# Two kinds of loads, of the mask and of the first part's maxima, moved from SyncE's queue to GpSimd's, in a two-layer transformer kernel

## The chip, the cores and the metric

The kernel runs on one core of a Trainium2 chip. The metric is the device time of one execution in microseconds (us). Three runs of the kernel before gave 3211.42, 3217.47 and 3217.95 us; the median is 3217.47.

The engines go by the names of the profile: PE is TensorE (matmuls), DVE is VectorE, ACT is ScalarE, POOL is GpSimd, SP is SyncE (no arithmetic, it begins transfers). Each runs its own list of instructions strictly in order and waits for the others by semaphores. L1034 is line 1034 of the kernel.

## The reference

The inputs are x (2048 rows of 256), a context of 1601 rows of 256, an integer mask of 2048 x 2048, and weights. Two layers follow each other, both with 16 heads of width 16:

```python
# layer 0 (x0, x1: the two halves of the rows; c: the context, whose first two rows give shifts, scales, gates)
x0 = x0 + gate * mha(mod(ln(x0)))          # self attention inside each half
x1 = x1 + gate * mha(mod(ln(x1)))
ox = attend(q of x0, k, v of x1);  oy = attend(q of x1, k, v of x0)
x  = x + gate * (proj(ox), proj(oy))       # cross attention between the halves
x  = x + gate * mlp(mod(ln(x)))            # gelu, width 1024
# layer 1
scores = where(mask == 0, -1e9, q @ k.T / 4)
x = layernorm(x + softmax(scores) @ v @ ow + ob)        # masked self attention over all 2048 rows
x = layernorm(x + mha(x, context, context))             # attention to the 1601 context rows
x = layernorm(x + relu(x @ w1 + b1) @ w2 + b2)
```

So there are four attentions, which the kernel calls stages 0 to 3: self, cross, masked, context. Only stage 2 has a mask.

## The kernel before

**Units and steps.** The rows of x make four blocks of 512 queries. Each stage runs through the blocks in the order of `ORDER` (stage 0: 0, 1, 2, 3; the others: 2, 3, 0, 1), and each block through four groups of four heads. One stage, block and group is a *unit*. Keys lie in two slots of 1024 (`slot`). The keys of a unit are walked in tiles of 128, two head pairs each; each such pair is a *step* of the main loop in `stream` (L1356 on). A step with one slot of the masked stage takes some 2 us, so a unit with 16 steps takes 32 us or more and one with 32 steps about 62.

Stage 2 begins when the cross stage has made only half of the keys. Its first block, block 2 (`SPLIT`), is therefore done in two *parts*: part 0 with the first slot of keys for groups 0 to 3, then part 1 with the second slot for groups 0 to 3. That makes eight units of 16 steps, and the results of the two parts are put together by `compare`, `invert_both`, `fetch_first` and `divide` (L1285 to L1324). These eight units run at about 1217 to 1575 us in the profiled execution; the last block of the cross stage, with its MLP, is finished beside them, and so are the four chunks of context (`chain_context`, L784), whose keys and values stage 3 needs.

**What a unit does.** Ahead of its turn, `maxima` (L1065) makes the scores once with queries on the partitions (PE, L1094 and L1099) and takes their maxima over the keys (DVE, L1109; in stage 2 L1102, which adds a row of the mask's bias first). `negated` and `as_rows` (L1116, L1129) turn the negative maxima into rows: PE L1133, then ACT L1138 writes `nm`. In its turn, `weights_of` (L1158) makes the scores with keys on the partitions: in stage 2 the bias, transposed, by L1173, the products by L1180, minus the maxima by L1187, then the exponential on ACT (L1194). `values_of` (L1198) multiplies by the values (L1211), `copy_sums` takes the sums out (L1243) and SP brings them to their places (L1249, L1258). Some steps later the reciprocal of the sums goes through memory (L1280, L1282) and `divide` multiplies on POOL (L1289, and L1292, L1293 where there are two parts).

**The order.** All five engines keep the order in which the code emits instructions (`manual_schedule`, L88); nothing is reordered. Work that lies beside the units is put in by hand: `later` is a list of functions with the number of steps until they are due, `background` a list of generators (the chains of normalization, projections, MLP) that are advanced one piece a step, `transfers` a list of loads of keys and values of which each step issues one (`load_ready`, L980).

**The two kinds of loads that the change touches.**

- `mask_rows` (L1016) loads 128 rows by 512 integers of the mask (256 KB) into `raw`, a tile with two buffers, and POOL turns it into a bias in bf16 (L1035). The load is L1034. There are 64 such pairs: eight for block 2 and slot 0, begun by `mask_part(0)` near the end of the cross stage; eight for block 2 and slot 1, begun by `mask_part(1)` during the down projection of the last cross MLP; and 16 for each of the blocks 3, 0 and 1, emitted between the maxima of the fourth group of the block before (L1082 to L1086), two by two or one by one.
- `as_rows` (L1129): for the eight units of block 2 alone, right after `nm` has been written, eight small loads (2 KB each, from two rows of `nm` per head to 32 partitions, L1145) bring the maxima into `mh`, and four steps later DVE adds the two halves (`add`, L1149 to L1151; the result serves `compare`).

**What else lies on POOL.** Sums with the gates and residuals of the layer (L586, L588; L599 later), the power of -1/2 in the normalizations (L400), the second part of the norms (L610), copies of weights (L230), a memset of a column of ones in each tile of values `v` (L506), the products of `divide` (L1289 to L1293). **What else lies on SP:** nearly all other transfers; for the steps of the prediction, the stores of keys and queries that have been split into two floats, `hi` and `lo` (L495), the stores of values (L542 to L550, each of which needs the memset and the sums of DVE, L523), the loads of keys (L933) and values (L949, L956), of queries (L1001) and of the context chunk (L793).

The tag `half` has three buffers for all of these: `hi`, `lo`, `sums`, `u`, `first`, `rd_first`. A `lo` (DVE, L486) therefore waits until an earlier store or an earlier product on POOL has let its buffer go. The values and w_raw share two buffers of `stage` in the same way.

Around the change the emission reads, in the main loop (L1453 on):

```python
                if masked:
                    second[s2]()
                take_maxima(step)
...
                after(step)
```

`take_maxima` emits the maxima that are due (and with them masks), and `after` what is due in `later`, one transfer and one piece of the background.

Of the kernel before, what the change touches and what calls it, by code (L numbers as in the profile page):

```python
# [22 lines left out]
P = 128  # L23
# [7 lines left out]
BLK = 512  # L31
# [45 lines left out]
def two_layers(ctx: ExitStack, tc: tile.TileContext, a: dict, out: bass.AP):  # L77
    nc = tc.nc
# [32 lines left out]
    def one_ps(dtype=F32, n=None):  # L111
        n = small[0] if n is None else n
        flush((n,))
        return ps.tile([P, BLK], dtype, tag=f"m{n}", bufs=1, name=f"m{n}_ps")
# [901 lines left out]
    def mask_rows(b, slot, qt, j):  # L1016

        if (b, slot, qt) not in bias_rows:
            if b != SPLIT:
                t = sb.tile([P, 2, SLOT], BF16, tag="w_mlp", bufs=WB, name="bias")  # L1020
                for s in range(2):
                    bias_rows[b, s, qt] = t[:, s, :]
            elif slot == 0:

                t = sb.tile([P, TPB, SLOT], BF16, tag="kT11", name="bias")
                for q in range(TPB):
                    bias_rows[b, slot, q] = t[:, q, :]
            else:
                t = sb.tile([P, 2, SLOT], BF16, tag="w_mlp", bufs=WB, name="bias")
                for q2 in range(2):  # L1030
                    bias_rows[b, slot, qt + q2] = t[:, q2, :]
        raw = sb.tile([P, BLK], I32, tag="raw", bufs=2, name="raw")
        q0, k0 = b * BLK + qt * P, KEYS[2][slot][j] * BLK
        nc.sync.dma_start(raw, a["mask"][q0 : q0 + P, k0 : k0 + BLK])  # L1034
        nc.gpsimd.tensor_scalar(  # L1035
            bias_rows[b, slot, qt][:, j * BLK : (j + 1) * BLK], raw, 0.0, MASKED,
            ALU.is_equal, ALU.mult,
        )

    def mask_part(slot):  # L1040

        for n in range(2 * TPB):
            later.append([n, lambda n=n: mask_rows(SPLIT, slot, n // 2, n % 2), False])
# [21 lines left out]
    def maxima(u):  # L1065
# [12 lines left out]
        def pair(qt, n, i):  # L1078
# [3 lines left out]
            if masked and i == 0 and g == NG - 1 and 1 in u["slots"]:  # L1082
                at = ORDER[2].index(b) + 1
                each = 2 * 2 // len(chunks)
                for j in range(n * each, (n + 1) * each) if at < NB else ():
                    mask_rows(ORDER[2][at], j // 2, qt, j % 2)  # L1086
# [42 lines left out]
    def as_rows(u):  # L1129

        m = one_ps()
        for qt in range(TPB):
            nc.tensor.matmul(  # L1133
                m[:, qt * P : (qt + 1) * P], lhsT=negpad[:, qt, :], rhs=identR,
                start=True, stop=True,
            )
        u["nm"] = sb.tile([P, BLK], F32R, tag="nm", bufs=2, name="nm")
        nc.scalar.copy(u["nm"], m)  # L1138
        if "part" in u:

            t = sb.tile([P, 2, 4 * BLK // P], F32, tag="mh", bufs=2, name="mh")
            for j in range(4):
                for h in range(2):
                    r = 64 * (j // 2) + 2 * (j % 2) + h
                    nc.sync.dma_start(  # L1145
                        t[PH * j : PH * (j + 1), h, :], u["nm"][r : r + 1, :].bitcast(F32)
                    )

            def add():  # L1149
                n = u["minus"] = part_tile(u, "minus")  # L1150
                nc.vector.tensor_tensor(n, t[:, 0, :], t[:, 1, :], ALU.add)  # L1151

            later.append([4, add, False])

    def part_tile(u, name):
        return sb.tile([P, 4 * BLK // P], F32, tag=f"{name}{u['g']}{u['part']}", name=name)
# [199 lines left out]
    def stream(stages, start_up):  # L1356
# [48 lines left out]
        def all_maxima(u):  # L1405
            negated(u)
            later.append([3, lambda: as_rows(u), True])
            if u.get("part") == 0 and u["g"] == NG - 1:
                want(2, 1, 1)
# [219 lines left out]
```

## Time and profile before

| | us |
|---|---|
| median of three runs | 3217.47 |
| the profiled execution's own time | 3220.77 |
| its span, first to last instruction | 3219.0 |
| PE busy | 2969.9 (92% of the span) |
| DVE busy | 2173.6 (68%) |
| ACT busy | 1719.3 (53%) |
| POOL busy | 389.1 (12%) |
| the 64 mask conversions on POOL (L1035) | 123.1, of 1.92 each |
| POOL's idle time that ended with a mask's landing | 243.7, in 38 waits |
| SP waiting for nm ahead of a maxima load (L1145) | 62.8, in 6 waits, the longest 32.4 |
| SP waiting for a conversion ahead of a mask load (L1034) | 57.2, in 33 waits |

All times come from one profiled execution. The time that the three runs took is measured without the profiler. In a timeline a line has the start in us from the first instruction, the length, the engine, the line of the code, the operation and its tiles; "x8" joins eight in a row, and brackets give the idle time before and what ended it. In the list of waits a line has who waited, for whom, then total, number and longest. For SP and its transfers the length is that of issuing, not of moving the data. Idle time of an engine matters only where PE, which is busy nearly all the time, has to stop for it.

The mean clock that PE was granted is 0.97 of full speed[...].

### The profile page before, as it was taken

To read this page: it belongs to the slowest core of one execution; us is meant where nothing else is said; L and a number is where in the kernel's file an instruction comes from. 1 tells how busy PE (TensorE), PEld (TensorE's weight loads), DVE (VectorE), ACT (ScalarE), POOL (GpSimd) and SP (SyncE) were. 2 spreads that over 40 slices of the span, in tenths; PEclk is the share of its full clock that TensorE was granted. 3 is DMA by queue.
4 is the path that set the end of the run, shared out by engine and by line. 5 is a ranking of instruction groups with operands and counts; after the bars stand their busy time and mean duration, and the time that the engine had idled before them with its cause. 6 is when DMAs were issued, how large, how long until landed. Compare 5 with 4: busy or idle time off the path is not lost.

```text
span 3219.0 us, 60012 instructions
## 1 busy us (share of the span) xinstructions
PE 2969.9 (92%) x24128; PEld 1453.8 (45%) x24128; DVE 2173.6 (68%) x3945; ACT 1719.3 (53%) x1897; POOL 389.1 (12%) x333
## 2 busy tenths in 40 slices
PE   7999999998999889898999999999989999999997
PEld 3444434444444345444555555554444444444443
DVE  5677777776666657476878878877667757657452
ACT  1465565565555536353555555555556546546462
POOL 0000101101010121204023013010010110110110
PEclk8999999999999999998999999999999999999998
DMA  7642261261114221354111011013240000101000
GB/s 217 134 87 87 60 103 58 65 123 29 62 28 98 50 86 38 97 99 125 46 52 54 18 42 59 19 29 72 43 107 20 19 18 20 26 19 28 11 14 18
DMA packets 177059, 191.39 MB, mean 59 GB/s; under 512 B 93940, under 2 KB 110844, under 8 KB 176780
## 3 DMA queue, kind: packets, MB, share of 16 engines
q1 hardware_dynamic: 175628, 187.55, 23.7%
q8 instruction: 190, 3.11, 0.4%
q14 instruction: 89, 0.73, 0.1%
q10 hardware_dynamic: 1152, 0.00, 0.0%
HBM read 129.78 MB, written 48.45 MB: 55 GB/s over the span
## 4 chain that ended last, share of the span: by engine, by line
PE 58%; DVE 6%; ACT 4%; DMA 4%; SPq 3%; issue 2%; POOL 1%; ACTq 0%; DVEq 0%; POOLq 0%
PE m_ps L1211 15%; PE s_ps L1180 12%; PE s_ps L1187 7%; PE s_ps L1099 5%; PE s_ps L1173 5%; PE m_ps L625 3%; ACT e L1194 3%; PE m_ps L678 3%; DVE s_ps L1102 2%; PE s_ps L1094 2%; DVE pm L1109 1%; PE m_ps L567 1%; PE m_ps L467 1%; DMA kT<-k_dr 1%; PE m_ps L513 1%
## 5 line engine op out<-in xcount | busy, mean ns | idle before, releaser
L1194 ACT ACTIVATE e<-s_ps 128x1024 f32<-128x1024 f32 (+1 forms) x1440 | 1467.0, 1024 | 1204.6 <-PE s_ps L1187 1195.0
L1109 DVE TENSOR_REDUCE pm<-s_ps 128x2 f32<-128x1024 f32 (+3 forms) x1024 | 1121.8, 1107 | 504.8 <-PE s_ps L1099 501.4
L1211 PE MATMUL m_ps<-e,V 128*32 128x256 f32 (+2 forms) x10432 | 913.0, 421 | 0.9 <-DVE lo L486 0.8
L1102 DVE CUSTOM_DVE_ANT_0 s_ps<-s_ps,bias 128x512 f32<-128x512 f32 x1024 | 712.7, 701 | 220.5 <-PE s_ps L1094 199.2
L1180 PE MATMUL s_ps<-q,kT 64*128 64x512 f32 (+1 forms) x2880 | 722.6, 498 | 28.2 <-ACT e L1194 23.2
L1099 PE MATMUL s_ps<-kT,q 64*128 64x512 f32 (+3 forms) x2560 | 603.0, 395 | 98.1 <-ACT e L1194 65.5
L1187 PE MATMUL s_ps<-nm,sel 64*128 64x512 f32 (+1 forms) x2880 | 576.0, 396 | 0.0
L1180 PEld LDWEIGHTS s_ps<-q,kT 64*128 64x128 f32 (+1 forms) x2880 | 270.1, 184 | 566.5 <-issue 402.5
L1099 PEld LDWEIGHTS s_ps<-kT,q 64*128 64x128 f32 x2560 | 294.1, 188 | 271.8 <-ACT e L1194 151.1
L1211 PEld LDWEIGHTS m_ps<-e,V 128*32 128x32 f32 (+1 forms) x10432 | 208.3, 109 | 348.0 <-issue 285.2
L1289 POOL TENSOR_TENSOR oT<-oT,rd_rows 64x512 f32<-64x512 f32 x63 | 80.2, 1274 | 1827.2 <-DMA rd_rows<-rd_dr 1356.4
L1187 PEld LDWEIGHTS s_ps<-nm,sel 64*128 64x128 f32 (+1 forms) x2880 | 276.6, 189 | 2.1
L1173 PE MATMUL s_ps<-biasT,ident 64*64 64x512 bf16 x2048 | 211.4, 403 | 8.3 <-DVE pm L1102 5.4
L1094 PE MATMUL s_ps<-kT,q 64*128 64x256 f32 x1024 | 206.4, 283 | 8.2 <-DMA kT<-k_dr 8.2
L1094 PEld LDWEIGHTS s_ps<-kT,q 64*128 64x128 f32 x1024 | 184.9, 185 | 30.5 <-DMA kT<-k_dr 8.4
L1173 PEld LDWEIGHTS <-ident 64*64 64x64 bf16 x2048 | 58.3, 103 | 231.3 <-issue 166.7
L1035 POOL TENSOR_SCALAR bias<-raw 128x512 bf16<-128x512 int32 x64 | 123.1, 1923 | 247.4 <-DMA raw<-in_mask 243.7
L1102 DVE DVE_READ_ACCUMULATOR2_ANT pm<- 128x1 f32 x1024 | 145.1, 142 | 0.0
L467 PE MATMUL m_ps<-hT,w_qk 128*128 128x512 f32 (+2 forms) x232 | 116.3, 625 | 9.4 <-DVE lo L486 8.3
L625 PE MATMUL m_ps<-hT,w_mlp 128*128 128x512 f32 x224 | 111.1, 618 | 5.8 <-ACT sums L1243 4.3
L486 DVE SCALAR_TENSOR_TENSOR lo<-m_ps,qkb,hi 128x512 fp32r<-128x512 f32 (+3 forms) x62 | 43.5, 701 | 104.8 <-ACT hi L485 59.5
L678 PE MATMUL m_ps<-w_mlp,hid 128*128 128x256 f32 x448 | 105.9, 390 | 0.0
(121 smaller groups left out, 1410.6 us busy)
## 6 DMA issues: line engine op xcount, KB each, us to landing
q<-q_dr SPq DMA_DIRECT2D x544, 64.0 KB
kT<-k_dr SPq DMA_DIRECT2D x192, 128.0 KB
raw<-in_mask SPq DMA_DIRECT2D x64, 256.0 KB
oT<-sums SPq DMA_DIRECT2D x256, 32.0 KB
rd_rows<-rd_dr SPq DMA_DIRECT2D x63, 128.0 KB
q_dr<-hi SPq DMA_DIRECT2D x30, 256.0 KB
q_dr<-lo SPq DMA_DIRECT2D x30, 256.0 KB
k_dr<-hi SPq DMA_DIRECT2D x24, 256.0 KB
```

The lines of the kernel that those rows point to most:

```text
L467: nc.tensor.matmul(m[:, :n], lhsT=wqk[:, k, w, c, :], rhs=hT[:, k, :n], start=k == 0, stop=k == 1)
L625: nc.tensor.matmul(m, lhsT=w1[k][:, f * P : (f + 1) * P], rhs=hT[:, k, :], start=k == 0, stop=k == 1,)
L678: nc.tensor.matmul(m[:, q2 * D : (q2 + 1) * D], lhsT=hid[f][:, qt * P : (qt + 1) * P], rhs=w2[f // 4][:, f % 4, :], start=f == 0, stop=f = ...
L1094: nc.tensor.matmul(exchanged(s[:, h, :], part), lhsT=queries, rhs=exchanged(keys, 1 - part), start=True, stop=True,)
L1099: nc.tensor.matmul(s[:, h, :nn], lhsT=queries, rhs=keys, start=True, stop=True)
L1102: nc.vector.tensor_tensor_reduce(out=s[:, h, :], in0=s[:, h, :], in1=bias_rows[b, slot, qt][:, c : c + nn], scale=1.0, scalar=-3.0e38, op0 ...
L1109: nc.vector.tensor_reduce(u["pm"][:, qt, :, i, n], s[:, :, :nn], AX.X, ALU.max)
L1173: nc.tensor.matmul(s[to : to + 64, h, :], lhsT=ident16[of : of + 64, of : of + 64], rhs=bias_columns[b, slot, kt][of : of + 64, :], start= ...
L1180: nc.tensor.matmul(s[:r, h, :], lhsT=kT[g][slot][64 * h : 64 * h + 64, i, kt * P : kt * P + r], rhs=u["q"][64 * h : 64 * h + 64, i, :], st ...
L1187: nc.tensor.matmul(s[:r, h, :], lhsT=sel[64 * h : 64 * h + 64, i, :r], rhs=u["nm"][64 * h : 64 * h + 64, :], start=False, stop=True,)
L1194: nc.scalar.activation(e[:r], s[:r], AF.Exp, scale=SCALE)
L1211: nc.tensor.matmul(u["av"][PH * j : PH * (j + 1), cut], lhsT=V[g][slot][:r, kt * GW + j * VW : kt * GW + j * VW + PH], rhs=u["e"][n, j % 2 ...
```

## The change

Two calls change the engine that begins the transfer, from `nc.sync` (SP) to `nc.gpsimd` (POOL): the mask load of `mask_rows` and the maxima load of `as_rows`. Nothing else changes: sizes, buffers, the place in the emitted order, and what waits for the data stay. SP begins all other transfers as before.

```diff
         raw = sb.tile([P, BLK], I32, tag="raw", bufs=2, name="raw")
         q0, k0 = b * BLK + qt * P, KEYS[2][slot][j] * BLK
-        nc.sync.dma_start(raw, a["mask"][q0 : q0 + P, k0 : k0 + BLK])
+
+        nc.gpsimd.dma_start(raw, a["mask"][q0 : q0 + P, k0 : k0 + BLK])
         nc.gpsimd.tensor_scalar(
             bias_rows[b, slot, qt][:, j * BLK : (j + 1) * BLK], raw, 0.0, MASKED,
             ALU.is_equal, ALU.mult,
@@
             for j in range(4):
                 for h in range(2):
                     r = 64 * (j // 2) + 2 * (j % 2) + h
-                    nc.sync.dma_start(
+                    nc.gpsimd.dma_start(
                         t[PH * j : PH * (j + 1), h, :], u["nm"][r : r + 1, :].bitcast(F32)
                     )
```

## Prediction

> **What bounds the kernel now.** Read first: the chain of waits on the page.
>
> ```profile
> PE 58%; DVE 6%; ACT 4%; DMA 4%; SPq 3%; issue 2%; POOL 1%; ACTq 0%; DVEq 0%; POOLq 0%
> ```
>
> TensorE (PE) sets the end; SP's queue and POOL are on the path for 4%. So the question is where. Second, busy time by stretch (from:to, length, busy of PE, PEld, DVE, ACT, POOL, then clock, DMA share, GB/s):
>
> ```profile
> 1160.00:1170.00 10.00, 1.02 (x3) 0.87 (x4) 2.10 (x3) 1.39 (x2) 6.82 (x4) 0.56 0.52 177
> 1360.00:1370.00 10.00, 3.82 (x21) 1.99 (x21) 1.52 (x4) 0.20 (x1) 0.00 (x0) 0.63 0.71 115
> 1510.00:1520.00 10.00, 5.09 (x37) 2.48 (x29) 4.63 (x12) 2.86 (x4) 5.28 (x4) 0.98 0.55 178
> 1750.00:2000.00 250.00, 247.76 (x2484) 129.31 (x2480) 202.05 (x546) 144.63 (x157) 44.52 (x27) 1.00 0.13 40
> ```
>
> Where masks for blocks 0 and 1 are made (1750 on), PE is idle 2.2 us in 250: nothing to win. PE's holes lie at 1150 to 1530. Third, PE's waits in 1140 to 1560:
>
> ```profile
> PE m_ps L513 <- DVE lo L486: 21.1, 5, 11.3
> PE s_ps L1094 <- DMA kT<-k_dr: 8.2, 2, 7.9
> PE m_ps L418 <- DMA c<-in_ctx: 5.2, 2, 3.2
> ```
>
> Behind each stands a transfer that SP began late. SP's waits in 1230 to 1560 say why:
>
> ```profile
> SPq L1145 <- ACT nm L1138: 51.9, 5, 32.4
> SPq L1034 <- POOL bias L1035: 15.9, 11, 2.0
> ```
>
> SP stands in order behind the maxima (L1145) and the mask (L1034). Fourth, SP's and then POOL's timeline around the end of the cross stage:
>
> ```profile
> 1265.78 0.42 SPq L1034 DMA_DIRECT2D raw<-in_mask  x1
> 1298.71 4.94 SPq L1145 DMA_DIRECT2D mh<-nm  x8
> 1303.69 5.26 SPq L1034 DMA_DIRECT2D raw<-in_mask  x3
> ```
> ```profile
> 1268.87 1.94 POOL L1035 TENSOR_SCALAR bias<-raw 128x512 bf16<-128x512 int32 x1 [12.99 <-DMA raw<-in_mask]
> 1306.68 1.92 POOL L1035 TENSOR_SCALAR bias<-raw 128x512 bf16<-128x512 int32 x1 [35.88 <-DMA raw<-in_mask]
> 1322.54 1.28 POOL L588 TENSOR_TENSOR t<-t,u 128x512 f32<-128x512 f32 x1
> 1332.51 0.21 POOL L506 MEMSET v<- 128x64 f32 x1
> ```
>
> A load takes 3.09 us from issue to conversion (1265.78 to 1268.87; elsewhere 1723.77 to 1726.57, 2.80); mean 2.95. The lines also give the order that both engines keep: one mask, eight maxima loads, three masks.
>
> **What the Trainium skill says.** "DMA: Bandwidth & Descriptors", section "Latency and other measured facts": first byte about 0.6 us from SP, about 1 us from GpSimd, whose cores write the descriptors. "Anatomy of one DMA", same page: a GpSimd transfer takes 2.0 us + bytes/436e3. "Issuing engines are not separate DMA queues", same page: spreading issue saves only sequencer time. The trace of before has no GpSimd transfer, so it shows neither price; SP's own 0.62 us per maxima load (4.94/8) it does show.
>
> **The change.** Sixty-four loads of 256 KB and 64 of 2 KB leave SP's queue and enter POOL's. SP loses 64 x 0.34 + 64 x 0.6 = 60 us of issue, and the waits above. Bytes are the same. What changes on POOL: load n+1 stands behind conversion n, so the two raw buffers no longer overlap, and everything on POOL after a load waits for its landing.
>
> *Price R of one mask on POOL.* Landing 2.95 + 0.4 (the skill's 1.0 less 0.6), conversion and gap 2.0, a wait 0.1: R = 5.45 us. Low end: 2.6 (skill's formula for 256 KB) + 2.0 = 4.6. High end: half of the loads as slow as the one that met other traffic (1471.49 to 1476.17, 4.68): 6.3. *Price M of one maxima load:* 0.62 + 0.4 = 1.0, from 0.6 (as on SP) to 1.2 (twice); eight are 8.0.
>
> *First eight masks, 1146 to 1180.* Today PE's 11.3 us hole comes from the k_dr store (1163.01) that sits on SP behind masks; without them it goes out at about 1154.8, 8 us earlier. But POOL starts at 1145.7 (end of L588), six masks take 6R = 32.7, then comes the memset of v: 1178.6. The v store on SP (L542) needs it and goes out at 1177.87 today. SP then holds the q stores, which free the buffers that lo needs. Gain given back: 0 (low end -4, high +6).
>
> *Maxima of group 1 of part 0.* nm is there at about 1251; POOL is done with them at 1259.1, and the pow of L400 behind them, today over at 1255.9, at 1260.2. The normalization waits: +4 (0.5 to 5).
>
> *Second eight masks, 1266 to 1332.* Mask 1; then POOL waits for nm (1298.6) and begins eight maxima loads, to 1306.7; three masks, 1323.0; L586 and L588, 2.65, 1325.7; two masks, 1336.6; L586 and L588, 1339.2. That last sum t is what PE transposes at L418, in order, today at 1325.43 (t is ready 1323.8). PE stops: +14 (6 to 20). Nothing covers it: today these sums slip in between masks that have landed.
>
> *Freed keys.* At 1356 SP spends 4.99 us on maxima ahead of the last three kT loads, which land at 1366 while PE waits 7.9. Gone, they go out 7 us earlier: -6.6. At 1400 the same delays kT, w_raw and c (L418 waits 2.0 at 1424, and a slower clock follows, estimated 2): -4.
>
> *Sixteen masks for block 3, 1443 to 1545.* POOL's timeline of before:
>
> ```profile
> 1476.17 3.94 POOL L1035 TENSOR_SCALAR bias<-raw 128x512 bf16<-128x512 int32 x2 [55.50 <-DMA raw<-in_mask]
> 1484.74 1.28 POOL L1289 TENSOR_TENSOR oT<-oT,rd_rows 64x512 f32<-64x512 f32 x1
> 1518.70 3.92 POOL L1035 TENSOR_SCALAR bias<-raw 128x512 bf16<-128x512 int32 x2 [2.59 <-DMA raw<-in_mask]
> 1522.68 0.21 POOL L506 MEMSET v<- 128x64 f32 x1
> ```
>
> Sixteen end at 1522.6. After: maxima (nm at 1443.3) to 1451.3; four masks and a memset, 1473.3; L1289 to L1293, which need `first` (about 1483.3), 1486; two masks, 1496.9; eight maxima loads, 1504.9; ten masks, 1559.4; memset; the last eight maxima loads (nm long there), 1567.6; landing 2.0, 1569.6. DVE waits for those at L1151, in order ahead of all its maxima. Today:
>
> ```profile
> 1543.85 0.17 DVE L1151 TENSOR_TENSOR minus<-mh 128x16 f32<-128x16 f32 x1
> ```
>
> So +25.8 (9 to 39). The v store behind the memset holds SP too (1560 against 1540.56), with the c load of the last context chunk behind it: 19 us, inside the same stop. The holes at 1470 to 1520 (2.8, 3.2, 6.1), which SP's freedom would close, lie before this stop and are swallowed.
>
> *The 32 masks for blocks 0 and 1: nothing.* POOL does seven, waits at L1289 until 1745.8 as now, then nine: 1795 against 1766.6. Cover: PE takes the block's first transposes (L1058) at 1827.4, and the next divide comes at 1798.75. With R over 9 the cover would be gone.
>
> Sum: 0 + 4 + 14 - 6.6 - 4 + 25.8 = +33. The profiled execution took 3220.77 us (span 3219.0 and 1.8 around it) and would take 3254; the median of the three runs is 3.3 lower: 3217.5 + 33 = 3250.5. Low ends: -4 + 0.5 + 6 - 10.6 + 9 = +1. High: 6 + 5 + 20 - 10.6 + 39 = +59.
>
> **Rivals.** (1) *POOL keeps up, slower SP was the trouble: faster.* If R is under 4.6 and M at most 0.6, POOL's lateness at L418 and L1151 shrinks away and SP's freedom shows: 8 at 1160, 6.6, 4, and 12 at 1470 to 1520, 31 at most; half of it gives 3202. For it: SP's waits of 52 and 16 us are real, and POOL is busy only 12%. Against: a quick landing on SP still took 2.80, so 4.8 with the conversion. (2) *Cancelled:* R near 4.6 to 5, 3217 to 3224. (3) *POOL's loads dearer than the high end:* R 6.3, M 1.2, 3276; for it, three loads in contended stretches took 3.35 to 4.68; the masks of block 3 come while 110 to 178 GB/s move. That the change misses its aim can't be: both queues show by name.
>
> **Chances.** About 0.2% (6.4 us) is what a measurement of this kernel can tell from no change. Forecast case (R 5 to 6) 0.5; rival 3, 0.2: slower 0.7. Rival 2 0.15, mostly same. Rival 1 0.15: faster. Range: from 3210, which leaves out most of rival 1, to 3278, the dear end.
>
> **What would show it.** In the changed trace: isolated mask loads 3.2 to 3.8 us before their conversion and POOL's masks 5.45 apart; PE waiting about 14 us at L418 for L588 near 1326 to 1340; the kT wait at 1358 down to about 1; DVE waiting some 25 us at L1151 for mh near 1545; no hole of PE in 1750 to 2000. Masks under 4.6 us apart make the prediction wrong; so does a last maxima load that DVE doesn't wait for.

## The result, and the profile after

The changed kernel takes 3236.49 us (median of eight runs, 3222.89 to 3243.62) against 3215.30 us before (median of eight). The two medians lie 21 us apart. The ratio is put at 1.0059, with a 95% interval of 1.0042 to 1.0076, which makes 19 us slower (13.5 to 24.4). The forecast was slower by 33 us. Its profiled execution took 3243.62 us, of which 3241.9 are the span; 22.9 more than the profiled execution before. The change adds a blank line, so lines from 1034 on have moved down by one: L1103 after is L1102 before.

The chain that ended last, after:

```profile
PE 58%; DVE 6%; ACT 4%; DMA 3%; issue 3%; POOL 2%; SPq 1%; ACTq 0%; POOLq 0%; DVEq 0%
```

SyncE's queue fell from 3% to 1% and GpSimd rose from 1% to 2%: the waiting has changed its engine. By stretch (from:to, length, busy of PE, PEld, DVE, ACT, POOL, clock, DMA share, GB/s):

```profile
1360.00:1370.00 10.00, 9.96 (x70) 4.02 (x66) 3.60 (x10) 4.57 (x6) 0.00 (x0) 1.00 0.63 193
1750.00:2000.00 250.00, 247.76 (x2483) 129.33 (x2480) 201.87 (x546) 144.69 (x156) 53.65 (x44) 1.00 0.13 40
```

TensorE's hole at 1360 is filled, and in 1750 to 2000 it is busy for the very same 247.76 us as before. TensorE's waits in 1140 to 1560, after (sum, times, longest):

```profile
PE m_ps L418 <- DMA c<-in_ctx: 17.6, 2, 17.4
PE m_ps L513 <- DVE lo L486: 8.4, 4, 4.2
PE m_ps L1134 <- DVE lo L486: 7.9, 1, 7.9
PE m_ps L418 <- POOL t L588: 7.9, 1, 7.9
```

The kT wait of 7.9 is gone from the top of the list. The hole behind `lo` has shrunk in one place (11.3 to 4.2) and come up in another (7.9 at L1134). The stop for t from L588 is new, and the one for c, 3.2 at the longest before, has grown to 17.4. The c load is SyncE's, but SyncE was not late by itself. Its waits in 1230 to 1560 held this line, where before they held 52 us at L1145 and 16 at the mask:

```profile
SPq L548 <- POOL v L506: 21.7, 1, 21.7
```

And VectorE's first wait in 1480 to 1560:

```profile
DVE minus L1152 <- DMA mh<-nm: 25.6, 2, 19.7
```

GpSimd's timeline shows why both come at once:

```profile
1543.56 1.93 POOL L1036 TENSOR_SCALAR bias<-raw 128x512 bf16<-128x512 int32 x1 [2.40 <-DMA raw<-in_mask]
1545.55 0.59 POOL L1035 DMA_DIRECT2D raw<-in_mask  x1
1548.51 1.93 POOL L1036 TENSOR_SCALAR bias<-raw 128x512 bf16<-128x512 int32 x1 [2.37 <-DMA raw<-in_mask]
1550.49 0.21 POOL L506 MEMSET v<- 128x64 f32 x1
1550.59 3.98 POOL L1146 DMA_DIRECT2D mh<-nm  x8
```

Load, 2.96 us until it has landed, conversion, next load: 4.96 us a mask. Behind the last of the sixteen masks for block 3 stand the memset (SyncE's v store and then the c load hang on it) and the last eight maxima loads (VectorE hangs on them). Before, the masks ended at 1522.6.

Following the same instruction through both traces says where the time went. VectorE's additions at L1151 (L1152) were late by 4.9, 5.4, 5.4, 5.7, 5.8, 0.1, 4.5 and 12.3 us, at 1227, 1262, 1323, 1378, 1412, 1459, 1496 and 1544 of before. The last of them, at 1543.85 before:

```profile
1556.17 0.18 DVE L1152 TENSOR_TENSOR minus<-mh 128x16 f32<-128x16 f32 x1 [19.73 <-DMA mh<-nm]
```

GpSimd's multiplication at L1289 (L1290) fills in the rest: it was 3.8 us late at 1101, ahead of the first moved load, 12.35 at 1578 and 16.05 at 3141. So some 3.7 us came in after 1578, where no wait of TensorE on a moved load was found. And then comes a term that the prediction did not have. The last VectorE instructions, before and after:

```profile
3214.78 0.88 DVE L830 SCALAR_TENSOR_TENSOR t<-t,rs,rows 128x256 f32<-128x256 f32 x2 [0.19 <-POOL rs L827]
```
```profile
3230.57 0.88 DVE L830 SCALAR_TENSOR_TENSOR t<-t,rs,rows 128x256 f32<-128x256 f32 x2 [0.19 <-POOL rs L827]
```

The spans end at 3219.0 and 3241.9, so 3.3 us lay between the last VectorE instruction and the end before, and 10.4 after.

### The profile page after: what moved, and what is told of

It reads as the page before. It is cut to its first block, busy times and chain, and to the rows that moved or that the text cites. A ratio compares the mean times of both kernels' runs of the same rounds, so it can differ in the third digit from the quotient of the medians.

```text
span 3241.9 us, 60034 instructions
## 1 busy us (share of the span) xinstructions
PE 2970.0 (92%) x24128; PEld 1451.7 (45%) x24128; DVE 2174.3 (67%) x3945; ACT 1719.8 (53%) x1897; POOL 458.6 (14%) x461
## 4 chain that ended last, share of the span: by engine, by line
PE 58%; DVE 6%; ACT 4%; DMA 3%; issue 3%; POOL 2%; SPq 1%; ACTq 0%; POOLq 0%; DVEq 0%
PE m_ps L1212 16%; PE s_ps L1181 12%; PE s_ps L1188 7%; PE s_ps L1100 5%; PE s_ps L1174 5%; ACT e L1195 3%; PE m_ps L625 3%; PE m_ps L678 3%; PE s_ps L1095 2%; PE m_ps L567 1%; DVE pm L1110 1%; DVE s_ps L1103 1%; PE m_ps L467 1%; POOL bias L1036 1%; PE m_ps L513 1%
## 5 line engine op out<-in xcount | busy, mean ns | idle before, releaser
L1103 DVE CUSTOM_DVE_ANT_0 s_ps<-s_ps,bias 128x512 f32<-128x512 f32 x1024 | 712.5, 700 | 215.4 <-PE s_ps L1095 193.7
L1290 POOL TENSOR_TENSOR oT<-oT,rd_rows 64x512 f32<-64x512 f32 x63 | 80.2, 1274 | 1757.1 <-DMA rd_rows<-rd_dr 1329.2
L1095 PEld LDWEIGHTS s_ps<-kT,q 64*128 64x128 f32 x1024 | 185.8, 186 | 23.2 <-DMA kT<-k_dr 1.5
L1103 DVE DVE_READ_ACCUMULATOR2_ANT pm<- 128x1 f32 x1024 | 144.6, 141 | 0.0
L467 PE MATMUL m_ps<-hT,w_qk 128*128 128x512 f32 (+2 forms) x232 | 116.6, 627 | 9.6 <-DVE lo L486 8.3
```

The lines of the kernel that those rows point to most:

```text
L1095: nc.tensor.matmul(exchanged(s[:, h, :], part), lhsT=queries, rhs=exchanged(keys, 1 - part), start=True, stop=True,)
L1103: nc.vector.tensor_tensor_reduce(out=s[:, h, :], in0=s[:, h, :], in1=bias_rows[b, slot, qt][:, c : c + nn], scale=1.0, scalar=-3.0e38, op0 ...
```

## The experiments

Times are set against the runs of the kernel before that shared the chip (medians 3218.35 for the first four, 3212.34 for the next four, 3217.84 for the last three). My theory at this point: GpSimd is late because each load waits behind the conversion before it, SyncE's freedom is a real gain, and the end costs a further 7 us. The rival: a load begun by GpSimd is dear by itself, wherever it stands and whatever its order.

**One mask load by GpSimd.**

```diff
+        last_mask = (b, slot, qt, j) == (ORDER[2][-1], 1, TPB - 1, 1)
+        eng = nc.gpsimd if last_mask else nc.sync
-        nc.sync.dma_start(raw, a["mask"][q0 : q0 + P, k0 : k0 + BLK])
+        eng.dma_start(raw, a["mask"][q0 : q0 + P, k0 : k0 + BLK])
```

> The kernel before with a single load moved: the very last of the 64 mask loads, in a stretch where TensorE never stops, is begun by GpSimd. Theory A (a fixed end cost: a program that uses GpSimd's queue at all ends later, as in the changed kernel, where 10.4 us lie between the last VectorE instruction and the end of the span against 3.3 before): about +7 us, 3222, ratio 1.002, and the same 10 us at the end of the trace. Theory B (the longer end belongs to the 128 loads, or to that one execution): no change, 3.3 us at the end.

Measured: 3216.73, ratio 0.9994 (0.9983 to 1.0006), 3.4 us at the end. A fixed cost of using the queue is refuted. The end still had to be explained.

**All masks, and nothing else.**

```diff
-        nc.sync.dma_start(raw, a["mask"][q0 : q0 + P, k0 : k0 + BLK])
+        nc.gpsimd.dma_start(raw, a["mask"][q0 : q0 + P, k0 : k0 + BLK])
```

> All 64 mask loads begun by GpSimd, the maxima loads left on SyncE. Theory A (each mask load waits on GpSimd's queue behind the conversion before it, 4.96 us a mask, and end cost of 7 us; the masks ahead of L588 no longer stand behind the maxima's wait; SyncE keeps its wait for nm): VectorE's two waits for mh (5.8 and 19.7 us) gone, the wait at L418 for c near 1550 of some 6 us, the kT wait of 7.9 us near 1360 back; +10 to +15 us against before, 3225 to 3230. Theory B (the masks alone are the whole cost): as the changed kernel, 3236, ratio 1.006.

Measured: 3229.21, ratio 1.0045 (1.0027 to 1.0064), +14.5: within theory A, but the stop at c was far above the 6 us expected. TensorE's first waits in 1140 to 1650:

```profile
PE m_ps L418 <- DMA c<-in_ctx: 25.5, 2, 22.8
PE s_ps L1094 <- DMA kT<-k_dr: 12.2, 2, 7.9
```

VectorE's waits for mh are gone and the kT hole is back, as expected; but the stop for c near 1550 is as long as ever. The late maxima loads were not needed for it.

**All maxima loads, and nothing else.**

```diff
-                    nc.sync.dma_start(
+                    nc.gpsimd.dma_start(
                         t[PH * j : PH * (j + 1), h, :], u["nm"][r : r + 1, :].bitcast(F32)
```

> The 64 maxima loads begun by GpSimd, the mask loads left on SyncE, two buffers deep. Theory A (a freed SyncE gains about 8 us at the kT wait near 1360 and about 5 us at the c load near 1424; the last maxima load stands behind sixteen masks that end near 1523 and is not late; end cost 7): -4 to -8 us against before, 3207 to 3211, ratio 0.998. Theory B (maxima loads on GpSimd are a cost of their own): slower than before by 5 us or more besides the 7.

Measured: 3202.13, ratio 0.9953 (0.9940 to 0.9967), -15: the sign of theory A, but about twice the gain that it asked (4 to 8). VectorE's additions come 10.2 us earlier between 1323 and 1378 (kT, expected 8) and 5.6 between 1412 and 1459 (c, expected 5), and the end costs 1.8 us where 7 were expected. TensorE's first waits, 1140 to 1650:

```profile
PE m_ps L513 <- DVE lo L486: 20.4, 5, 11.8
...
PE s_ps L1094 <- DMA kT<-k_dr: 0.9, 1, 0.9
```

Half of the change is a gain by itself. What stays is the hole near 1160 (11.8), where the k_dr store stands on SyncE behind mask loads.

**Load n+1 ahead of conversion n.** Both kinds of loads on GpSimd, the same two buffers; `mask_order` lists the 64 masks in the order of the calls, and `raws` the tiles whose loads have been begun. The lines without a sign are as before, the first two moved into the loop:

```diff
+        while len(raws) <= min(mask_order.index((b, slot, qt, j)) + 1, len(mask_order) - 1):
+            mb, ms, mq, mj = mask_order[len(raws)]
             raw = sb.tile([P, BLK], I32, tag="raw", bufs=2, name="raw")
+            q0, k0 = mb * BLK + mq * P, KEYS[2][ms][mj] * BLK
             nc.gpsimd.dma_start(raw, a["mask"][q0 : q0 + P, k0 : k0 + BLK])
+            raws.append(raw)
+        raw = raws[mask_order.index((b, slot, qt, j))]
         nc.gpsimd.tensor_scalar(
```

> The changed kernel, with GpSimd beginning load n+1 ahead of conversion n, in the same two buffers. Theory A (the serial load and conversion is what makes GpSimd late): masks about 2.6 us apart instead of 4.96, the waits at L418 for t (7.9) and c (17.4) and for mh (19.7) nearly gone, SyncE's gain kept, the end cost kept: 3205 to 3213 against 3236, 23 to 31 us less than the changed kernel. Theory B (the loads by GpSimd are slow or disturb VectorE and TensorE whatever their order): 3230 or more.

Measured: 3183.62, ratio 0.9901 (0.9875 to 0.9926), -32 against before and some 50 less than the changed kernel. GpSimd near 1490:

```profile
1489.75 0.58 POOL L1042 DMA_DIRECT2D raw<-in_mask  x1 [0.30 <-POOL bias L1045]
1490.41 1.93 POOL L1045 TENSOR_SCALAR bias<-raw 128x512 bf16<-128x512 int32 x1
1492.63 0.58 POOL L1042 DMA_DIRECT2D raw<-in_mask  x1 [0.30 <-POOL bias L1045]
```

2.88 us a mask in place of 4.96: the landing lies beside the conversion. The waits for t, c and mh are gone (none over 0.4 us is left of mh), and TensorE's longest sum of waits in 1140 to 1650 is now small:

```profile
PE m_ps L513 <- DVE lo L486: 7.5, 5, 3.1
```

Theory A holds in kind and was too small in size: at L1151 this kernel is 8.5 us early by 1227, 17.9 by 1378, 23.6 by 1459 and 36.9 by 1544.

**The 32 masks for blocks 0 and 1.**

```diff
+        eng = nc.gpsimd if b in ORDER[2][2:] else nc.sync
-        nc.sync.dma_start(raw, a["mask"][q0 : q0 + P, k0 : k0 + BLK])
+        eng.dma_start(raw, a["mask"][q0 : q0 + P, k0 : k0 + BLK])
```

> The kernel before with the last 32 mask loads (for blocks 0 and 1) begun by GpSimd. Theory A (in 1680 to 2100 TensorE has cover for a mask every 5 us; GpSimd's queue is drained at the end at 0.083 us a load, 64 loads took 5.4 and 128 took 10.6 us, beside the 3.3 us that the output takes anyway, so 32 loads, 2.7 us, cost nothing): within 2 us of before, 3.3 to 3.5 us at the end. Theory B (loads by GpSimd cost wherever they stand): a quarter to a half of the masks-only run's 14.5 us, 4 to 7 us slower.

Measured: 3211.16, ratio 0.9994 (0.9985 to 1.0003), 3.4 us at the end. Theory A: the cover that the prediction named holds.

**Every mask load in two halves**, in the prefetching kernel.

```diff
-            nc.gpsimd.dma_start(raw, a["mask"][q0 : q0 + P, k0 : k0 + BLK])
+            for r in range(0, P, P // 2):
+                nc.gpsimd.dma_start(
+                    raw[r : r + P // 2], a["mask"][q0 + r : q0 + r + P // 2, k0 : k0 + BLK]
+                )
```

> The prefetching kernel with every mask load cut in two of 64 rows: 192 loads by GpSimd in place of 128, the same bytes, twice as many issues per mask. Theory A (the end of GpSimd's queue costs 0.083 us for each load): 192 x 0.083 = 16 us from the last VectorE instruction to the end of the span, 5.4 more than with 128. Theory B (it goes by bytes or packets, which stay the same): 10.5 us as with 128.

Measured: 3182.58 in a single run, which says little of the time, with 5.8 us at the end. Both theories missed the end: it is shorter with more loads. The run of 129 loads below asks why.

**Masks only, memset of v on VectorE.**

```diff
-        nc.gpsimd.memset(by_head[:, :, :, HD:], 1.0)
+        nc.vector.memset(by_head[:, :, :, HD:], 1.0)
-        nc.sync.dma_start(raw, a["mask"][q0 : q0 + P, k0 : k0 + BLK])
+        nc.gpsimd.dma_start(raw, a["mask"][q0 : q0 + P, k0 : k0 + BLK])
```

> Mask loads by GpSimd, maxima loads by SyncE, and the memset of v (L506) on VectorE in place of GpSimd. Theory A (the stop of 22.8 us at L418 near 1540 comes only through the memset behind sixteen masks, the v store that needs it and the c load behind that on SyncE): the stop under 4 us, 17 to 22 us less than masks only, 3207 to 3213. Theory B (the v store was not the cause: the bias rows or the mask loads' traffic hold TensorE): a stop of over 10 us stays, 3220 or more.

Measured: 3211.91, ratio 0.9997 (0.9988 to 1.0005), 15 us less than masks only by the ratios, close to theory A (17 to 22 less). But the trace says that the stop moved rather than went, which is theory B's sign. TensorE no longer waits at L418 beyond 2.4 us; it waits 14.5 at L467 for `lo`, and VectorE in 1480 to 1560:

```profile
DVE lo L486 <- POOL first L1292: 15.3, 1, 15.3
```

L1292 stands behind the same row of masks. So the chain through the memset was the cause of the wait for c, and with it gone GpSimd's lateness reaches VectorE by another way, with a stop of 14.5 in place of 22.8. Half of the gain has another place, which the next run shows.

**The changed kernel, memset of v on VectorE.**

```diff
-        nc.gpsimd.memset(by_head[:, :, :, HD:], 1.0)
+        nc.vector.memset(by_head[:, :, :, HD:], 1.0)
```

> The changed kernel (masks and maxima by GpSimd) with the memset of v on VectorE. Theory A (two causes share one stop near 1550: the c load behind the memset, and VectorE's wait for the last maxima, which alone is 19.7 us): TensorE no longer waits at L418 for c, but VectorE still waits 15 to 20 us at the maxima, and the time stays within 8 us of the changed kernel, 3228 to 3237. Theory B (the memset is the whole cost): 15 us less or more, 3222 or under.

Measured: 3226.09, ratio 1.0039 (1.0024 to 1.0053), 6 us less than the changed kernel by the ratios, whose intervals overlap. VectorE in 1480 to 1560:

```profile
DVE minus L1151 <- DMA mh<-nm: 26.8, 2, 21.0
```

Theory A: in the changed kernel two causes share one stop, and taking one away leaves the other at full length. What this kernel gains, it gains near 1180, where the memset stands behind six of the first eight masks, and SyncE's v store behind the memset. That store in the changed kernel, and here:

```profile
1183.61 0.60 SPq L542 DMA_DIRECT2D v_dr<-v  x1
```
```profile
1170.96 0.60 SPq L542 DMA_DIRECT2D v_dr<-v  x1
```

Counted from GpSimd's multiplication at 1101, which lies ahead of every moved load, VectorE's addition at 1227 is 1.1 us late in the changed kernel and 10.4 us early here; of these 11.4 us, 8.5 are left at 1578. Between the two masks-only kernels the difference is 11.7 us at 1227 and 23.2 at 1578: half of it comes from the early memset and not from the stop near 1550.

**129 loads in place of 128.** The prefetching kernel, the last mask load as two of 64 rows.

```diff
+            for r in range(0, P, P // 2 if len(raws) == len(mask_order) - 1 else P):
+                n = P // 2 if len(raws) == len(mask_order) - 1 else P
+                nc.gpsimd.dma_start(
+                    raw[r : r + n], a["mask"][q0 + r : q0 + r + n, k0 : k0 + BLK]
+                )
-            nc.gpsimd.dma_start(raw, a["mask"][q0 : q0 + P, k0 : k0 + BLK])
```

> The prefetching kernel with the last of the mask loads cut in two of 64 rows, so that GpSimd begins 129 transfers in place of 128; nothing else. The drain that ends GpSimd's work took 0.60, 1.09, 3.53, 6.14 and 11.36 us with 0, 1, 32, 64 and 128 loads, but only 6.71 us with 192. Theory A (what is drained is counted in laps of 128: 192 counts as 64, and 129 as 1): a drain of about 1 us, 3.4 us from the last VectorE instruction to the end, and 7 us less than the prefetching kernel, 3175 to 3180. Theory B (halved loads drain more cheaply, or the queue empties itself during long runs): a drain of about 11 us, 10.4 at the end, 3183 as there.

Measured: 3178.31, ratio 0.9884 (0.9863 to 0.9905), the lowest ratio of all, though its interval overlaps that of the prefetching kernel; 3.3 us at the end where that has 10.5. DRAIN is the name in the profile of instructions that close an engine's list. GpSimd's, booked to the line that opens the program, for before, 32 loads, 64 (masks only), 128 (the changed kernel, then prefetching), 192 (halves) and 129 (number, then shortest/median/longest in ns, first and last start):

```profile
L1625 POOLq DRAIN  x3: 34/77/603, 3214.2 to 3218.7; - x3
```
```profile
L1626 POOLq DRAIN  x3: 40/102/3529, 3208.9 to 3213.7; - x3
```
```profile
L1625 POOLq DRAIN  x3: 40/102/6142, 3227.3 to 3234.0; - x3
```
```profile
L1626 POOLq DRAIN  x3: 46/93/11364, 3229.7 to 3241.6; - x3
```
```profile
L1635 POOLq DRAIN  x3: 46/98/11367, 3178.4 to 3190.3; - x3
```
```profile
L1638 POOLq DRAIN  x3: 46/93/6712, 3173.3 to 3180.5; - x3
```
```profile
L1639 POOLq DRAIN  x3: 46/93/1567, 3170.6 to 3175.4; - x3
```

Read the longest: 0.6, 3.5, 6.1, 11.4 and 11.4 us, then 6.7 and 1.6. Theory A. The drain grows by (11.37 - 3.53)/96 = 0.082 us a load up to 128, and 129 loads drain nearly like one (1.6 against 1.1 us). The number of loads counts and not their bytes: 64 maxima loads of 2 KB take 6.1 us too (maxima only). The drain begins with GpSimd's last work and runs beside the last output, so 32 loads show nothing, 64 show 2 us and 128 show 7. In this run GpSimd also paused between its 128th load and its 129th, with nothing in the profile to wait for:

```profile
1980.17 0.54 POOL L1044 DMA_DIRECT2D raw<-in_mask  x1 [2.79 <-issue]
```

**Masks ahead on GpSimd, maxima on SyncE.** Against the prefetching kernel:

```diff
-                    nc.gpsimd.dma_start(
+                    nc.sync.dma_start(
                         t[PH * j : PH * (j + 1), h, :], u["nm"][r : r + 1, :].bitcast(F32)
```

> Mask loads by GpSimd with load n+1 ahead of conversion n, maxima loads left on SyncE. Theory A (two separate gains of a freed SyncE: one from the masks, once GpSimd is not late, one from the maxima, which maxima only gave as 15 us with 1.9 of end cost paid): kT's 7.9 us near 1360 and c's wait near 1424 come back, the 11 us hole near 1160 does not; 8 to 18 us less than before, ratio 0.9945 to 0.9975, and 10 to 20 more than the prefetching kernel. Theory B (all of the gain is the maxima's, the masks by GpSimd only cost less): no faster than before.

Measured: 3197.10, ratio 0.9942 (0.9920 to 0.9964), -19. Theory A; its drain is 6.1 us. TensorE's first waits, 1140 to 1650:

```profile
PE s_ps L1104 <- DMA kT<-k_dr: 9.9, 2, 7.7
PE m_ps L513 <- DVE lo L486: 7.6, 5, 3.3
```

The hole that the maxima make (7.7) is here, the one that the masks make (11.3 before) is not. The two halves are separate gains, and they add up: without their ends (1.8, 1.8 and 7.1 us more than before) masks ahead gains 20.5, maxima only 16.9, and the prefetching kernel, which has both, 39.0.

**Maxima loads by ScalarE.**

```diff
-                    nc.sync.dma_start(
+                    nc.scalar.dma_start(
                         t[PH * j : PH * (j + 1), h, :], u["nm"][r : r + 1, :].bitcast(F32)
```

> The kernel before with the maxima loads begun by ScalarE, which has just written nm itself, in place of SyncE. Theory A (the gain of maxima only is SyncE's, whoever takes the loads; ScalarE has slack for 8 issues of some 0.6 us, busy 53 percent, though exponentials wait behind them, 2 us of it seen by TensorE each time; no GpSimd drain): between before and maxima only, 5 to 17 us less than before. Theory B (exponentials behind 5 us of issue stop TensorE in each of eight groups by 3 us or more): no faster than before.

Measured: 3216.33, ratio 0.9996 (0.9981 to 1.0010). No gain: theory B in the time, though its price was not 3 us in each group. ScalarE's timeline:

```profile
1211.12 5.09 ACTq L1145 DMA_DIRECT2D mh<-nm  x8
1216.25 0.59 ACT L1063 COPY biasT<-m_ps 128x512 bf16<-128x512 bf16 x1 [5.16 <-DMA mh<-nm]
```

ScalarE does nothing else for 5 us, and the longest TensorE wait for an exponential in 1140 to 1650 grew from 1.1 to 3.4 us. SyncE, too, now waited 17.3 us in 1230 to 1560 at kT loads (L933), by the profile's account for maxima loads to land. Which of the two took the larger part of the gain wasn't tried.

## Why the prediction was right, and where it was off

The sign, the mechanism and the places were right: GpSimd falls behind because a load stands behind the conversion before it, and sixteen masks for block 3 carry the loss. The prefetching kernel shows it by reversal: same queues, same transfers, same buffers, another order, and the loss becomes a gain of 32 us. The size was off in several terms that partly cancel, and part of the total is luck: the stretch that the prediction worked out, 1101 to 1578, costs 8.5 us where 33 were forecast, and 7.1 more come from the end of the program, which the forecast had at nothing. With R at 4.96, rival 2's case (R near 4.6 to 5, a time of 3217 to 3224) came true in the price, and it is the end that takes the time well clear of it: 3236.5 less 7.1 would be 3229.

- **R**, 5.45 forecast, is 4.96 in quiet stretches (up to 6.9 in the first masks, where other traffic flows). The extra 0.4 us for a GpSimd load, taken from the first-byte figures of the Trainium skill ("DMA: Bandwidth & Descriptors", "Latency and other measured facts"), did not show: 2.96 from issue to conversion, against 2.95 taken from SyncE's loads. The first byte by itself no run here shows; for the whole load the measurement decides.
- **M**, 1.0 forecast, is 0.50 (3.98 for eight): cheaper than SyncE's 0.62, and below the range of 0.6 to 1.2.
- **First eight masks**, forecast 0: the 11.3 us hole became 4.2 and 7.9, and the drift from 1101 to 1227 is 1.1. The reason given, a gain of SyncE's that the memset behind the masks gives back, is shown too: with the memset on VectorE the gain stays, 10.3 and 10.4 us by 1227 in the two runs.
- **Maxima ahead of L400**, forecast +4: the pow began at 1260.42, 5.6 us later than before where the whole stretch was 4.9 late. About 0.7, since M was half.
- **L588 to L418**, forecast +14: TensorE waits 7.9, ending at 1338.89. The place is right. From nm to t GpSimd took 34.5 us where the forecast had 40.6: the 6 us between are those of R and M.
- **Freed kT and c**, forecast -6.6 and -4: the kT wait fell from 7.9 to 1.0, and the lateness by 5.6 between 1412 and 1459. The granted clock in 1420 to 1440, 0.83 before, is 1.00 after, which the estimate of a slower clock after the wait for c had claimed.
- **Sixteen masks for block 3**, forecast +25.8: VectorE waited 5.8 and 19.7 at L1152, and the lateness grew by 12.2 from 1459 to 1544. The last maxima load was issued by 1554.6 and not 1567.6; R and M account for that. That the c load hangs in the same stop was said, and the runs with the memset moved show it: the c wait vanishes and the mh wait of 21.0 stays. It also held the other way: without mh, c alone made 22.8 (masks only).
- **The last 32 masks**, forecast 0: 0.9994 when they alone are moved.
- **The end**, not in the forecast at all: +7.1 us (10.4 less 3.3). The prediction took the stretch after the last computation as fixed. The profile of before could not show it, for it had no transfer begun by GpSimd to drain.

Added: from 1101 to 1578 the trace gives 12.35 - 3.8 = +8.5 where the forecast had +33, and the end gives +7.1; together 15.6 of the measured 19 (13.5 to 24.4). The other 7 us of the 22.9 between the two profiled executions lie where no changed instruction holds TensorE, and I leave them to the spread of single executions (3222.89 to 3243.62 for this kernel; in the nine other runs whose code is the same up to there, the multiplication at 1101 comes between 3.8 us earlier and 2.4 later than before).

Rival 1 had weighed SyncE's freedom at 31 us at most (8 at 1160, 6.6, 4, and 12 at 1470 to 1520). It was wrong for this kernel and nearly right as a figure: once GpSimd loads ahead, those very holes close, in steps of 9.5 (1101 to 1227), 10.3 (1323 to 1378), 5.6 (1412 to 1459) and 13.4 us (1496 to 1544), and the addition at 1544 is 36.9 us early.

## What to carry to other kernels

Moving loads to the engine that consumes them frees the issuing queue, but in an in-order engine it also puts each load behind the work on the load before it: begin the next load ahead of that work, or two buffers do the work of one. Count what stands behind the row of loads on the new engine (here a memset of 0.21 us and eight loads of 2 KB). Where two waits share a stop, taking one away only shows the other, as near 1550; where one stands alone, taking it away is a gain, as the 10 us near 1180. And look at the end of the program, not only at its stages: the time between the last computation and the end of the span is part of the time.

## What was not expected of the hardware

GpSimd's drain at the end of the program grows with the transfers that it began: 0.60 us with none, 1.09 with one, 3.53 with 32, 6.14 with 64, 11.36 with 128. With 192 it takes 6.71 and with 129 it takes 1.57. Laps of 128 describe all seven values to within 0.6 us; what is being drained, and whether the lap is always 128, no run here shows. Both runs with more than 128 have a pause of GpSimd right after its 128th transfer for which the profile names no other engine, of 0.31 us with 192 and of 2.79 us with 129.
